# Expert attention of a two-layer token model: the order of TensorE's work within a pair, and gates one pair earlier

## Chip, cores and metric

The kernel runs on one core of one Trainium2 chip. The metric is the device time of one execution in microseconds (us). The kernel before takes 2606.87 us, the median of three runs (2605.61 to 2609.41).

## What is computed

The model takes 128 images through a tokenizer, two attention and feed-forward layers, and an expert layer. The change lies in the first feed-forward part, here called expert attention. Cut to what matters, it computes for `x` of 128 images, 64 tokens and 256 features:

```python
xn = layernorm(x) * norm_w
gate = softmax(xn @ router_w.T + router_b)          # 4 experts
xc = xn.reshape(B, T, C, DC)                        # 4 chunks of 64 features
q, k, v = einsum('btcd,ekd->btcek', xc, qkv_w)      # per chunk, expert and head (2 heads of 32)
attn = softmax(einsum('bcehtd,bcehsd->bcehts', q, k) * scale)
y = einsum('bcehts,bcehsd->bcehtd', attn, v)
y = einsum('btced,eod->btceo', y, proj_w) + proj_b
out = einsum('btceo,bte->btco', y, gate).reshape(B, T, D)
x = x + out @ out_w.T
```

All of it is in float32.

## The kernel before, in words

**Tiling.** Two images make a pair of 128 rows; there are 64 pairs, numbered p. The stream of activations, `h2`, stays on chip. Four pairs make a block, which is normalized and transposed together (class `Block`, 16 of them); what belongs to a single pair is in class `Pair`. The projection of each expert is folded into the values' weights, so a pair needs queries, keys, values, scores, softmax, the product with the values and one output product.

**Steps of a pair.** On TensorE: `queries_keys` (L1014, 64 matmuls in two halves, 64x64 tiles of the array), `values` (L1034, 64 matmuls in two halves, 64x64), `scores` (L1059, 128 matmuls, 32x64), the transposes of the attention weights (L1096, 16, 128x128), `mixed`, the product of values and weights (L1109, 64, 128x64), and `output` (L1125, 4, 128x128). On VectorE: `maxima` (L1069), `less_max` (L1073), `sums` with a reciprocal (L1079, L1080), half of the values' copies out of PSUM (L1048) and `added`, which adds the output product to the stream (L1129). On ScalarE: the copies of queries and keys (L1020), of the transposed weights (L1099), of `mixed` (L1120), of the other half of the values (L1046), and the exponents (L1076). On GpSimd: `weights`, a small product of reciprocal sums and gates (L1086) and a large one with the exponents (L1087).

**Three pairs at once.** The loop in `rest` handles three pairs in iteration p: `cur` (p) from its scores to its weights, `old` (p-1) from the transposes of its weights to the addition, and `new` (p+1), whose queries, keys and values are made. Pair 0 runs beside the end of the previous stage in `first`.

**Steps of a block.** These are spread over the iterations before the block's first pair n by a table, `work`, keyed by iteration and place. `at(...)` fills it and `do((p, place))` writes out what stands there. They are the statistics on VectorE ("DVE", at n-11 and n-10); on GpSimd ("POOL") the factors (L885 to L897, nine small operations, at n-9) and one normal with its stream each (L913 and L921, at n-8 to n-5); the transposes (L936) with their ScalarE copies; the logits of the router (L956, its copy L966, its transpose L971); and the gates' softmax (L976 to L988), which ends in `gates` on GpSimd.

**What sets the order.** The whole stage stands in a `manual_schedule`, so each engine runs its instructions in the order in which they are written; an instruction waits for what it reads and for the buffer it writes. PSUM has two areas here. One, `pss`, has two buffers of two banks for the scores (`sc`). The other, `sh.ps`, is one ring of four one-bank buffers that all other products share in order.

Of the kernel before, what the change touches and what calls it, by code (L numbers as in the profile page):

```python
# [12 lines left out]
F32 = mybir.dt.float32  # L13
# [7 lines left out]
P = 128  # L21
B = 128
T = 64
D = 256
# [266 lines left out]
class Shared:  # L291
# [13 lines left out]
    def ps(self, shape, name):  # L305
        return self.psq.tile(shape, F32, tag="pq", name=name)
# [455 lines left out]
def expert_attention(c, sh, front, hd, normw, wr, br, wqkv, wvT, wproj, bproj, wout):  # L762
# [4 lines left out]
    tc, nc, h2 = c.tc, c.nc, c.h2  # L767
# [3 lines left out]
    ps, small = sh.ps, sh.small  # L771
# [64 lines left out]
    wt = Weights()  # L836
# [15 lines left out]
    class Block:  # L852
# [4 lines left out]
        def __init__(self, p0):  # L857
            self.p0 = p0
            self.b = p0 // NB
# [78 lines left out]
        def transposed(self, fc):  # L938
            if fc == 0:
                self.xT = row(self.b)[:, NB * D :].rearrange("p (c n t) -> p c n t", c=2, n=NB)  # L940
            nc.scalar.activation(self.xT[:, fc], self.pt, AF.Copy, scale=nw[:, fc : fc + 1])
# [48 lines left out]
    class Pair:  # L990
# [4 lines left out]
        def __init__(self, p, blk):  # L995
            self.p, self.n, self.blk = p, p % NB, blk
            self.xT = blk.xT[:, :, p % NB, :]
            self.e, self.sm, self.pT = {}, {}, {}
            self.v = None

            qk = ring(sh.bp, "k", [P, 2, 16, T])
            self.qk = qk.rearrange("p (c a e t) -> p c a e t", c=4, a=2, e=2)

        def queries_keys(self, fc):

            self.pq = pq = [ps([P, 2, 2, P], "pqk") for _ in range(2)]
            for k in range(2):
                for eh in range(2):
                    for half in range(2):
                        o = slice(half * 64, half * 64 + 64)  # L1010
                        for par in range(2):
                            r = slice(par * 64, par * 64 + 64)
                            f = k * D + eh * P + half * 64
                            nc.tensor.matmul(  # L1014
                                pq[par][o, k, eh, :], wt.w[r, f : f + 64], self.xT[r, fc], start=True, stop=True
                            )

        def queries_keys_copied(self, fc, copy=nc.scalar.copy, pars=range(2)):
            for par in pars:
                copy(self.qk[:, 2 * fc + par], self.pq[par])  # L1020

        def values(self, h):

# [62 lines left out]
            eng.tensor_mul(s2, s2, bcast(self.blk.gate[:, self.n, x::2], 1, 8))  # L1086
            eng.tensor_mul(e, e, bcast(sm, 2, T))  # L1087

        def transposed(self, x):
            e = self.e.pop(x)  # L1090
            self.pT[x] = pT = self.pools.ep.tile([P, 2, 4, P], F32, tag="pT", name="pT")
            for h in range(2):
                pt = ps([P, 4, P], "pt")
                for cq in range(4):
                    i = h * 8 + cq * 2
                    nc.tensor.transpose(  # L1096
                        pt[:, cq, :], e[:, i : i + 2, :].rearrange("p e s -> p (e s)"), c.ident
                    )
                nc.scalar.copy(pT[:, h], pt)  # L1099

        def mixed(self):

# [48 lines left out]
    def at(n, place, f, *a):  # L1151
        key = (n, place) if n >= 0 else "first"
        work.setdefault(key, []).append(lambda: f(*a))

    for b, x in enumerate(blocks):
        n = NB * b
        if b > 2:
            at(n - 11, "DVE", x.statistics, 0)
            at(n - 10, "DVE", x.statistics, 2)
        if b > 1:  # L1160
            at(n - 9 + 2 * (b == 2), "POOL", x.factors)
            for k in range(NB):
                at((1, 2, 2, 3)[k] if b == 2 else n - 8 + k, "POOL", x.normal, k)
        elif b == 1:
            for k in range(NB):
                at(1 + k // 2, "ACT2", x.stream_scalar, k)
        if b:
            at(n - 4, "PE", x.transpose, 0)
            at(n - 3, "ACT", x.transposed, 0)
            at(n - 3, "PE", x.transpose, 1)  # L1170
            at(n - 2, "ACT", x.transposed, 1)
            at(n - 2, "PE", x.logits_in_strips)
            at(n - 1, "ACT", x.logits_copied)
            at(n - 1, "PE", x.logits_transposed)
            at(n, "DVE0", x.logits_less_max)
            at(n, "ACT1", x.exponents)
            at(n, "DVE1", x.sums)
            at(n, "POOL0", x.gates)

    def do(key):  # L1180
        for step in work.pop(key, ()):
            step()
# [7 lines left out]
    pairs = {}  # L1190
# [6 lines left out]
    x, y, z = blocks[:3]  # L1197
# [31 lines left out]
    def first(cur, new, chunk, last):  # L1229

        new.queries_keys(0)
        chunk.exponents()
        new.queries_keys_copied(0)
        chunk.sums()
        chunk.weights()
        cur.scores()
        cur.maxima(0)
        cur.less_max(0)
        y.normal_scalar(0)
        new.queries_keys(1)  # L1240
        cur.maxima(1)
        cur.less_max(1)
        chunk.transpose()
        new.queries_keys_copied(1)
        chunk.transposed()
        cur.exponents(0)
        last.outcome(0)
        last.outcome(1)
        for par in range(2):
            last.outcome_copied(0, par)  # L1250
        cur.sums(0)
        cur.weights(0)
        cur.exponents(1)
        for par in range(2):
            last.outcome_copied(1, par, nc.vector.tensor_copy)
        cur.sums(1)
        cur.weights(1)
        new.values(0)
        new.values_kept(0)
        last.back(0)  # L1260
        last.back(1)
        last.added(0)
        last.added(1)
        for k in range(1, 4):
            y.normal_scalar(k)
        new.values(1)
        new.values_kept(1)
        last.back(2)
        last.back(3)
        last.added(2)  # L1270
        last.added(3)
        sh.end.close()
        front.open()
        for k in range(NB):
            x.stream(k)
        do((0, "POOL"))
        do((0, "PE"))

    def rest(chunk, last):
        with (  # L1280
            tc.tile_pool(name="fe", bufs=4) as ep,
            tc.tile_pool(name="fps", bufs=2, space=PSUM) as pss,
            tc.manual_schedule(),
        ):
            Pair.pools = SimpleNamespace(ep=ep, pss=pss)
            old, cur = None, pairs[0]
            for p in range(NP):
                new = Pair(p + 1, blocks[(p + 1) // NB]) if p + 1 < NP else None
                if p == 0:
                    first(cur, new, chunk, last)  # L1290
                    old, cur = cur, new
                    continue
                if p == 8:
                    front.weights()
                do((p, "ACT"))
                do((p, "DVE0"))
                cur.scores()
                do((p, "DVE"))
                for x in range(2):
                    cur.maxima(x)  # L1300
                for x in range(2):
                    cur.less_max(x)
                do((p, "ACT1"))
                do((p, "DVE1"))
                do((p, "POOL0"))
                for x in range(2):
                    old.transposed(x)
                if new:
                    new.queries_keys(0)
                    new.queries_keys_copied(0, pars=(0,))  # L1310
                old.mixed()
                cur.exponents(0)
                if new:
                    new.queries_keys_copied(0, pars=(1,))
                old.mixed_copied()
                cur.sums(0)
                if new:
                    new.values(1)
                    new.queries_keys(1)
                cur.exponents(1)  # L1320
                if new:
                    new.values_kept(1)
                    new.queries_keys_copied(1)
                cur.weights(0)
                do((p, "ACT2"))
                old.output()
                if not new:
                    c.busy(ps([P, 2 * D], "idle"), wt.w, 3)
                cur.sums(1)
                cur.weights(1, nc.gpsimd if new else nc.vector)  # L1330
                do((p, "PE"))
                do((p, "POOL"))
                if new:
                    new.values(0)
                    new.values_kept(0)
                old.added()
                old, cur = cur, new
            for x in range(2):
                old.transposed(x)
            old.mixed()  # L1340
            old.mixed_copied()
            old.output()
            old.added()
        assert not work
# [1004 lines left out]
```

## Time and profile before

| what | value |
|---|---|
| median of three runs | 2606.87 us |
| profiled execution, its own time | 2605.81 us |
| its span, first to last instruction | 2604.1 us |
| mean granted TensorE clock | 0.989 |
| scores of pair 0 to scores of pair 63 | 1083.3 to 1800.4 us |
| large weights product on GpSimd (L1087) | 127 of 1902 ns |
| exponents on ScalarE (L1076) | 128 of 1062 ns |
| transposed-weight copies on ScalarE (L1099) | 256 of 599 ns |
| query and key copies on ScalarE (L1020) | 254 of 583 ns |

In the profile, PE is TensorE, DVE is VectorE, ACT is ScalarE, POOL is GpSimd, and PEld is TensorE's loading of weights. A line of the timeline holds the start in us from the first instruction, the duration, the engine, the line of the kernel, the operation, the tile written and the tiles read, the shape, and how many neighbouring instructions are merged (x32). A bracket at the end gives the engine's idle time before it and what ended it. A line of a stretch holds its length, the busy time of PE, PEld, DVE, ACT and POOL with their instruction counts, then the mean granted TensorE clock (1.00 is full speed), the share of DMA and its GB/s. Each float32 product appears as two matmul instructions, while a transpose is one.

### The profile page before, as it was taken

To read this page: it belongs to the slowest core of one execution; us is meant where nothing else is said; L and a number is where in the kernel's file an instruction comes from. 1 tells how busy PE (TensorE), PEld (TensorE's weight loads), DVE (VectorE), ACT (ScalarE), POOL (GpSimd) and SP (SyncE) were. 2 spreads that over 40 slices of the span, in tenths; PEclk is the share of its full clock that TensorE was granted. 3 is DMA by queue.
4 is the path that set the end of the run, shared out by engine and by line. 5 is a ranking of instruction groups with operands and counts; after the bars stand their busy time and mean duration, and the time that the engine had idled before them with its cause. 6 is when DMAs were issued, how large, how long until landed. Compare 5 with 4: busy or idle time off the path is not lost. (4 is left out here: it accounts for less than half of the span.)

```text
span 2604.1 us, 85832 instructions
## 1 busy us (share of the span) xinstructions
PE 2487.1 (96%) x37681; PEld 1697.3 (65%) x37681; DVE 2004.8 (77%) x3000; ACT 1632.2 (63%) x3421; POOL 1626.7 (62%) x1428
## 2 busy tenths in 40 slices
PE   8989999999999999899999999999999968999997
PEld 4554444444444444588888888887566557888886
DVE  5759999999999999888888888877567785444443
ACT  2228899898898888776776676665444533323232
POOL 3419999899898999676666676752233313454443
PEclk9999999999999999999999999999999989999998
DMA  3100000000000000000000000000344444555554
GB/s 115 33 13 1 2 2 2 2 2 1 2 2 1 2 13 2 3 29 14 25 14 25 14 24 14 24 14 26 81 101 99 94 113 178 189 189 191 192 193 133
DMA packets 138063, 141.45 MB, mean 54 GB/s; under 512 B 108002, under 2 KB 121860, under 8 KB 129871
## 3 DMA queue, kind: packets, MB, share of 16 engines
q1 hardware_dynamic: 128684, 119.48, 15.4%
q0 software_dynamic: 7648, 14.77, 1.8%
q8 instruction: 297, 4.87, 0.8%
q10 hardware_dynamic: 1344, 1.61, 0.2%
q14 instruction: 90, 0.73, 0.1%
HBM read 104.00 MB, written 32.54 MB: 52 GB/s over the span
## 5 line engine op out<-in xcount | busy, mean ns | idle before, releaser
L540 POOL TENSOR_TENSOR m<-q,k 128x1024 f32<-128x1024 f32 x384 | 719.6, 1907 | 55.4 <-PE sc L342 46.7
L532 DVE TENSOR_TENSOR m<-pc,k 128x2048 f32<-128x2048 f32 (+1 forms) x320 | 646.6, 2056 | 0.5 <-ACT q L472 0.5
L342 PE MATMUL sc<-m,wide 128*32 128x512 f32 x4096 | 520.1, 597 | 8.9 <-ACT m L541 6.6
L541 ACT ACTIVATE m<-m 128x1024 f32<-128x1024 f32 x384 | 402.4, 1049 | 20.5 <-POOL m L540 20.5
L342 PEld LDWEIGHTS sc<-m,wide 128*32 128x32 f32 x4096 | 134.7, 109 | 269.4 <-issue 157.9
L550 ACT ACTIVATE m<-k,q 128x64 f32<-128x64 f32 x1024 | 270.7, 338 | 0.9 <-DVE k L419 0.9
L1087 POOL TENSOR_TENSOR e<-e,mx 128x1024 f32<-128x1024 f32 x127 | 241.6, 1902 | 9.9
L1069 DVE TENSOR_REDUCE mx<-sc 128x16 f32<-128x1024 f32 x128 | 150.9, 1220 | 93.0 <-PE sc L1059 90.0
L2175 PE MATMUL ph<-xt,w1s 128*128 128x256 f32 x896 | 200.7, 382 | 2.1 <-DVE xt L2166 1.3
L2191 PE MATMUL po<-w2s,hT 128*128 128x256 f32 x896 | 198.0, 379 | 0.0
L2175 PEld LDWEIGHTS ph<-xt,w1s 128*128 128x128 f32 x896 | 171.0, 191 | 27.3 <-ACT hT L2179 2.0
L2191 PEld LDWEIGHTS po<-w2s,hT 128*128 128x128 f32 x896 | 168.1, 190 | 21.7
L1020 ACT COPY kr<-pqk 128x512 f32<-128x512 f32 x254 | 141.4, 583 | 56.8 <-PE pqk L1014 56.6
L1086 POOL TENSOR_TENSOR mx<-mx,gate 128x16 f32<-128x16 f32 x127 | 27.4, 215 | 235.2 <-DVE mx L1080 213.2
L1099 ACT COPY pT<-pt 128x512 f32<-128x512 f32 x256 | 132.1, 599 | 65.5 <-PE pt L1096 65.2
L1079 DVE TENSOR_REDUCE mx<-e 128x16 f32<-128x1024 f32 x128 | 155.0, 1211 | 11.4 <-ACT e L1076 9.6
L2209 POOL DMA_INDIRECT out<-y,rout x56 | 56.6, 1010 | 168.2 <-ACT hT L2179 119.2
L2179 ACT ACTIVATE hT<-ph,w1s 128x256 f32<-128x256 f32 x224 | 93.0, 470 | 98.6 <-PE ph L2175 95.1
L1073 DVE TENSOR_TENSOR e<-sc,mx 128x1024 f32<-128x1024 f32 x128 | 150.3, 1215 | 0.1
L2196 ACT ACTIVATE y<-y,gf 128x256 f32<-128x256 f32 x56 | 28.0, 507 | 195.0 <-issue 114.8
L1076 ACT ACTIVATE e<-e 128x1024 f32<-128x1024 f32 x128 | 136.0, 1062 | 1.1 <-DVE e L1073 0.7
L1109 PE MATMUL pz<-pT,vr 128*64 128x64 f32 x4096 | 134.7, 224 | 1.1 <-issue 0.7
(337 smaller groups left out, 4949.5 us busy)
## 6 DMA issues: line engine op xcount, KB each, us to landing
w1s<-in_we SPq DMA_DIRECT2D x30, 1028.0 KB
w2s<-in_we SPq DMA_DIRECT2D x30, 1024.0 KB
h<-hd SPq DMA_DIRECT2D x4, 2048.0 KB
hx<-h SPq DMA_DIRECT2D x4, 2048.0 KB
out<-h SPq DMA_DIRECT2D x4, 2048.0 KB
xt<-in_x SPq DMA_DIRECT2D x15, 512.0 KB
hd<-h SPq DMA_DIRECT2D x15, 512.0 KB
x<-hd SPq DMA_DIRECT2D x12, 512.0 KB
```

What stands on the lines that cost most here:

```text
L342: nc.tensor.matmul(dst[j : j + 32], wide[:, hf, s : s + 32], part, start=start, stop=stop)
L532: nc.vector.tensor_tensor(m, bcast(self.pq[:, hf, i : i + n], 3, T), k, ALU.max)
L540: nc.gpsimd.tensor_tensor(m, bcast(self.q[:, hf, s : s + 2], 3, T), k, ALU.subtract)
L541: nc.scalar.activation(m, m, AF.Relu)
L550: nc.scalar.activation(self.parts[i, hf][:, q], self.blk.k[:, hf, i], AF.Relu, bias=self.q[:, hf, i - NB // 2, q : q + 1], scale=-1.0,)
L1020: copy(self.qk[:, 2 * fc + par], self.pq[par])
L1069: nc.vector.tensor_reduce(mx, self.sc[x].rearrange("p h c s -> p (h c) s"), AX.X, ALU.max)
L1073: nc.vector.tensor_sub(e, self.sc[x].rearrange("p h c s -> p (h c) s"), bcast(self.sm[x], 2, T))
L1079: nc.vector.tensor_reduce(self.sm[x], self.e[x], AX.X, ALU.add)
L1087: eng.tensor_mul(e, e, bcast(sm, 2, T))
L2175: nc.tensor.matmul(ph[:, j], self.w1[:, w0 : w0 + P], self.xt[:, fc], start=(fc == 0), stop=(fc == 1))
L2191: nc.tensor.matmul(po, self.hT[:, f, r * P : r * P + P], self.w2[:, f, :], start=(f == 0), stop=(f == 7))
```

## The change

The iteration is written in another order, and four things move with it.

- The output product and the addition of a pair move one iteration later: a third pair, `older` (p-2), is carried for it.
- Queries and keys use the two-bank buffers of the scores when they are made in the loop, both halves one after the other.
- The transposes of the weights are split into the TensorE part (`transposes`) and the ScalarE copy (`transposed`), written alternately. Block work on TensorE comes right after them.
- In the table of block steps, the second transposed copy and the logits' copy are written one iteration earlier, each in the iteration of its TensorE step, and the gates' softmax moves from iteration n to n-1. GpSimd's block work (`POOL`), which was written after the weights of the pair, is now written ahead of them and behind the gates; VectorE's statistics (`DVE`) move from ahead of the maxima to the end of the iteration.

```diff
-        def queries_keys(self, fc):
-            self.pq = pq = [ps([P, 2, 2, P], "pqk") for _ in range(2)]
+        def queries_keys(self, fc, among_scores=False):
+            if among_scores:
+                pq = self.pools.pss.tile([P, 2, 2, 2, P], F32, tag="sc", name="pqk")
+                pq = [pq[:, par] for par in range(2)]
+            else:
+                pq = [ps([P, 2, 2, P], "pqk") for _ in range(2)]
+            self.pq[fc] = pq
...
-            at(n - 4, "PE", x.transpose, 0)
-            at(n - 3, "ACT", x.transposed, 0)
-            at(n - 3, "PE", x.transpose, 1)
-            at(n - 2, "ACT", x.transposed, 1)
+            for fc in range(2):
+                at(n - 4 + fc, "PE", x.transpose, fc)
+                at(n - 4 + fc, "ACT", x.transposed, fc)
             at(n - 2, "PE", x.logits_in_strips)
-            at(n - 1, "ACT", x.logits_copied)
+            at(n - 2, "ACT", x.logits_copied)
             at(n - 1, "PE", x.logits_transposed)
-            at(n, "DVE0", x.logits_less_max)
-            at(n, "ACT1", x.exponents)
-            at(n, "DVE1", x.sums)
-            at(n, "POOL0", x.gates)
+            at(n - 1, "DVE0", x.logits_less_max)
+            at(n - 1, "ACT1", x.exponents)
+            at(n - 1, "DVE1", x.sums)
+            at(n - 1, "POOL0", x.gates)
...
-                do((p, "ACT"))
-                do((p, "DVE0"))
                 cur.scores()
-                do((p, "DVE"))
                 for x in range(2):
                     cur.maxima(x)
                 for x in range(2):
                     cur.less_max(x)
+                for x in range(2):
+                    for h in range(2):
+                        old.transposes(x, h)
+                        old.transposed(x, h)
+                do((p, "PE"))
+                do((p, "ACT"))
+                do((p, "DVE0"))
+                if older:
+                    older.output()
+                old.mixed()
+                cur.exponents(0)
+                cur.exponents(1)
                 do((p, "ACT1"))
                 do((p, "DVE1"))
                 do((p, "POOL0"))
-                for x in range(2):
-                    old.transposed(x)
-                if new:
-                    new.queries_keys(0)
-                    new.queries_keys_copied(0, pars=(0,))
-                old.mixed()
-                cur.exponents(0)
-                if new:
-                    new.queries_keys_copied(0, pars=(1,))
-                old.mixed_copied()
-                cur.sums(0)
-                if new:
-                    new.values(1)
-                    new.queries_keys(1)
-                cur.exponents(1)
-                if new:
-                    new.values_kept(1)
-                    new.queries_keys_copied(1)
-                cur.weights(0)
+                do((p, "POOL"))
+                cur.sums(0)
+                cur.weights(0)
+                if older:
+                    older.added()
+                old.mixed_copied()
+                if new:
+                    for fc in range(2):
+                        new.queries_keys(fc, True)
+                        new.queries_keys_copied(fc)
+                else:
+                    c.busy(ps([P, 2 * D], "idle"), wt.w, 3)
                 do((p, "ACT2"))
-                old.output()
-                if not new:
-                    c.busy(ps([P, 2 * D], "idle"), wt.w, 3)
                 cur.sums(1)
                 cur.weights(1, nc.gpsimd if new else nc.vector)
-                do((p, "PE"))
-                do((p, "POOL"))
                 if new:
-                    new.values(0)
-                    new.values_kept(0)
-                old.added()
-                old, cur = cur, new
+                    for h in (1, 0):
+                        new.values(h)
+                        new.values_kept(h)
+                do((p, "DVE"))
+                older, old, cur = old, cur, new
```

After the loop, the transposes of the last pair, the output of the one before it, and then the rest of the last pair follow.

## The prediction, made before the changed kernel was run

> **What bounds the kernel now.** I read the page first, then the stretch of this stage alone, then one pair on TensorE, then the other engines in that pair. The stage runs 64 iterations of one loop; the scores of pairs 2 and 63 start at 1111.6 and 1800.4 us.
>
> ```profile
> PE 2487.1 (96%) x37681; PEld 1697.3 (65%) x37681; DVE 2004.8 (77%) x3000; ACT 1632.2 (63%) x3421; POOL 1626.7 (62%) x1428
> ```
> ```profile
> 1111.60:1800.40 688.80, 671.86 (x21126) 594.37 (x21122) 577.51 (x846) 482.24 (x854) 444.65 (x502) 1.00 0.07 20
> 1892.60:1896.10 3.50, 0.02 (x1) 0.00 (x0) 3.47 (x6) 2.98 (x6) 3.50 (x3) 1.00 0.00 0
> 1896.10:1899.60 3.50, 3.48 (x11) 2.95 (x12) 3.47 (x5) 2.81 (x4) 0.71 (x1) 0.52 0.36 60
> ```
> The first stretch is 61 pairs: 688.8/61 = 11.29 us a pair, TensorE busy 671.86 of 688.80, the others far less. TensorE bounds it. (The other two lines, from a later stage, are for the clock.)
>
> ```profile
> 1507.56 1.60 PE L1059 MATMUL sc<-kr 32*64 32x64 f32 x128
> 1509.08 1.97 PE L1096 MATMUL pt<-ident,e 128*128 128x128 f32 x16
> 1510.98 1.10 PE L1014 MATMUL pqk<-xnr,xTr 64*64 64x128 f32 x32
> 1512.01 2.21 PE L1109 MATMUL pz<-pT,vr 128*64 128x64 f32 x64
> 1514.15 1.10 PE L1034 MATMUL pv<-xTr,xnr 64*64 64x128 f32 x32
> 1515.08 1.05 PE L1014 MATMUL pqk<-xnr,xTr 64*64 64x128 f32 x32
> 1516.06 1.13 PE L1125 MATMUL po<-xTr,z 128*128 128x256 f32 x4
> 1517.03 0.60 PE L936 MATMUL ptx<-ident,xTr 128*128 128x128 f32 x4
> 1517.56 1.10 PE L1034 MATMUL pv<-xTr,xnr 64*64 64x128 f32 x32
> 1518.59 0.66 PE L1059 MATMUL sc<-kr 32*64 32x64 f32 x37
> ```
> One iteration, 11.03 us, without an idle bracket. Starts can be subtracted, modelled ends can't. The same 32 values matmuls take 0.93 us where the same tile shape follows (1514.15 to 1515.08) and 1.03 where another follows (1517.56 to 1518.59): 0.10 us is the price of a change of shape. There are seven changes an iteration.
>
> ```profile
> 1509.12 2.36 DVE L1069 TENSOR_REDUCE mx<-sc 128x16 f32<-128x1024 f32 x2 [0.72 <-PE sc L1059]
> 1511.39 2.35 DVE L1073 TENSOR_TENSOR e<-sc,mx 128x1024 f32<-128x1024 f32 x2
> 1513.79 1.22 DVE L1079 TENSOR_REDUCE mx<-e 128x16 f32<-128x1024 f32 x1
> ```
> ```profile
> 1403.19 1.90 POOL L1087 TENSOR_TENSOR e<-e,mx 128x1024 f32<-128x1024 f32 x1
> 1405.08 1.23 POOL L913 TENSOR_SCALAR oTr<-h,mv,rs 128x256 f32<-128x256 f32 x1
> 1406.40 1.23 POOL L921 TENSOR_SCALAR h<-h,rs,mr 128x256 f32<-128x256 f32 x1
> 1407.60 0.20 POOL L885 TENSOR_TENSOR rs<-mv,eps 128x4 f32<-128x4 f32 x1
> ...
> 1411.34 0.20 POOL L897 TENSOR_TENSOR rs<-rs,one 128x4 f32<-128x4 f32 x1
> 1411.53 0.21 POOL L988 TENSOR_TENSOR gate<-gate,gm 128x16 f32<-128x16 f32 x1
> 1412.92 0.21 POOL L1086 TENSOR_TENSOR mx<-mx,gate 128x16 f32<-128x16 f32 x1 [1.18 <-ACT e L1076]
> ```
> VectorE shows the chain behind the scores: counted from their start, maxima begin at +1.56 and both subtractions are done at +6.2. GpSimd shows the key fact: in every fourth iteration it has 6.45 us of block work (1405.08 to 1411.53: one normal with its stream, 2.5 us, and the factors, 3.9), which fits between the weights of one pair and of the next. The gates (L988) come after it and, in that trace, find their sums long done.
>
> **The order on TensorE.** After the change an iteration runs scores, transposes, block work, output of the pair before last, mixed, both queries_keys, both values. Seven changes of shape become four: transposes to keys, keys to mixed and keys to output are gone. 3 x 0.10 = 0.30 us. The wait of the output for its z (0.08 to 0.14 us, one pair in four) goes too: 0.33 us a pair. In the pair with logits in strips (128x32) two changes come back, 0.2 once in four. Over 62 pairs: 62 x 0.33 - 15 x 0.2 = 17, and about 2 us of one-time GpSimd waits early in the stage: **-19 us**. Here the Trainium skill bears on it: TensorEngine Tiling (Array Packing), Tiling Modes, says a change of mode drains the array, and TensorE: Matmul & The Clock Gate, Single matmul latency, gives about 166 ns for such a fill and drain. That would make 3 x 0.166 x 62 = 31 us (an estimate from the page). The row measures 0.10 for just this, so I take 19 and keep 31 for the range.
>
> The trace also has idle labelled "issue" on TensorE, mostly inside the scores (9.1 us in 14 cases at L1059). I keep it as is. Small matmuls now lie together before the scores; it could vanish or double (-13 to +13 us).
>
> **Does the new order wait by itself?** Offsets in a common iteration of 10.65 us: scores 0 to 1.5, transposes to 3.3, block 3.8, output 4.8, mixed 6.9, keys 8.7, values 10.65. ScalarE copies pT by 4.3 (before mixed), a block copy 5.0, exponents 5.1 to 7.35, z 7.7, four key copies 7.85 to 10.0 (1.07 us for two): ready 0.6 before the next scores. The keys' PSUM waits for the subtractions, done at 5.0 and 6.2, needed at 6.9 and 7.75. Sums on VectorE end at 7.7 and 9.5; the weights on GpSimd at 10.0 and 12.2; transposes need them at 12.2 and 13.1. Statistics, moved to the end, fill VectorE's idle time before the maxima. Nothing waits, with 0.6 to 1 us to spare: zero. The four-buffer ring serves 10 or 11 tiles an iteration instead of 14 or 15, all evacuated in time. The added step moves some 8 us later with its store on SP's queue and the loads behind it; nobody waits for those until the next stage, and in the last pair both adds still lie near the end: 0 (bounds -1 to +2).
>
> **The gates, one iteration earlier.** In iterations p = 3 mod 4 the gates now stand on GpSimd ahead of the block work, and that ahead of weights(0). They wait for a chain: the gate exponents stand on ScalarE behind both exponents (done +7.35, so +7.6), the gate sums on VectorE wait for them (done +8.05; queued behind: sums(0) and all after it), gates +8.1 to +8.3. GpSimd, idle since +1.6, only now starts its 6.45 us: done +14.8. weights(0) e runs 15.1 to 17.0, weights(1) 17.3 to 19.2 (2.16 us from one to the next). They were due at 12.2 and 13.1. The next iteration starts at 10.35 (the short logits transpose), its scores end at 11.9, and TensorE stands: first transposes 17.1 to 18.1, second 19.3 to 20.2, where 13.7 was due. **6.5 us a time.** Then it goes on at its pace: the block copy ends at 21.7, exponents 22.8 and 23.9, keys copied 26.9, scores 27.5; the weights of that pair are ready at 26.6 and 28.8 for 29.1 and 30.0. Nothing is caught up, TensorE is the bound.
>
> How often: GpSimd shows this long block before a gate 13 times in the stage (p = 3, 7 to 51). At p = 55 only the normal is left (2.5 us): weights 13.1 and 15.3, stall 2.5. At p = 59 nothing is queued, and only the later sums count: 1.3. Sum 13 x 6.5 + 3.8 = 88 us; some 3 us of "issue" idle hides in it: **+85 us**.
>
> **The clock.** A rule speaks against such a stall: TensorE: Matmul & The Clock Gate, HAM oscillation, says that an idle gap of over about 3.4 us halves the clock. The trace agrees: after 3.50 us of idle (second line of the stretches) the granted clock was 0.52 in the next 3.5 us, and eight L1505 matmuls took 3.20 us instead of 1.99 and 1.89. Here the gap is 5.2 us. By the rule, one 3.4 us window at half rate costs 1.7 us of work; but after restarting TensorE has only 0.95 us of transposes and then waits for weights(1) until 19.3, so much of the slow window lies under that wait. I take 1.0 a time, **+13 us**; bounds 0 and 2.5 (two windows), 0 to +33.
>
> **Sum**, against the profiled execution (span 2604.1, its own time 2605.8, 1.1 below the median): -19 + 85 + 13 = +79. From the median 2606.9: **2686**.
>
> **Rivals.**
> (a) Faster, 2586 (10%): GpSimd's detour stays off the path. It would have to finish its block work by about +9, as if started when idle at +1.6 (end +8.1). Against it: the gates' wait is in the written order, and the trace before keeps that order on every engine. Break-even is 19/15 = 1.3 us of stall per block; at +14.8 the work is 6 us too late. With only the late sums costing (15 x 1.3 = 19) the time would be unchanged.
> (b) Clock lost for two windows each time, "issue" idle doubled: 2686 + 20 + 13 = 2719 (12%). For it: a 7.0 us idle stretch early in the trace is followed by 6.8 us at half clock.
> (c) The keys' copies on ScalarE come late for the scores, since they stand behind the exponents and share the scores' two PSUM buffers: 0.5 us a pair, +31: 2717 (8%). Against it: 0.6 us to spare.
> (d) Stalls of 4 to 5 us, because block work runs faster or the gate chain is shorter than I walked: 2655 (10%).
>
> The likeliest, 60%: 2686. A measurement tells some 0.2% (5.2 us) from no change. Faster 0.08, same 0.02, slower 0.90; the range 2645 to 2720 leaves out (a) and half of (b) and (c).
>
> **What would show it.** Right: pairs of about 10.7 us where nothing waits; one start-to-start of about 17 in four; transposes (L1096 before) waiting for GpSimd's e for some 6 us, 13 times; gates waiting for VectorE, the block work after them; clock at 0.5 after these. Wrong: no GpSimd wait before the transposes; scores waiting for ScalarE's key copies; pairs of 11 us in spite of four changes of shape.

## The result, and the profile after

The changed kernel takes 2697.31 us (median of 4 runs, 2690.68 to 2701.89) against 2607.69 us before: ratio 1.0342, 95% interval 1.0317 to 1.0367. The predicted time was 2686. The profiled execution of the changed kernel took 2701.89 us, the longest of its four, and that of the kernel before 2605.81; so their traces lie 96 us apart, where the medians lie 90.

First the totals on the page of the changed kernel, then its stretches: the stage from the scores of pair 1 to those of pair 63, and one iteration with p = 28 (a multiple of 4). The columns are length, busy PE, PEld, DVE, ACT and POOL, and the granted clock.

```profile
PE 2507.4 (93%) x37681; PEld 1732.7 (64%) x37681; DVE 2012.0 (75%) x3000; ACT 1638.1 (61%) x3421; POOL 1624.5 (60%) x1428
```
```profile
1102.30:1896.80 794.50, 702.45 (x21471) 637.78 (x21470) 594.93 (x862) 496.22 (x868) 446.91 (x509) 0.93 0.06 17
1450.70:1468.50 17.80, 13.27 (x355) 11.96 (x352) 9.99 (x15) 8.42 (x14) 13.21 (x20) 0.81 0.01 2
```

The 62 iterations take 794.5 us where they took 700.2 (from 1100.2 to 1800.4 in the trace before); the rest of the kernel is unchanged within 1 to 2 us. So the whole difference lies in the loop. The iteration of 17.8 us has TensorE busy for 13.3 only, at a mean clock of 0.81. Here is TensorE in it:

```profile
1450.70 1.20 PE L1064 MATMUL sc<-kr 32*64 32x64 f32 x90
1452.17 0.69 PE L1064 MATMUL sc<-kr 32*64 32x64 f32 x38 [0.26 <-issue]
1456.94 1.97 PE L1100 MATMUL pt<-ident,e 128*128 128x128 f32 x8 [4.09 <-POOL e L1092]
1459.09 1.97 PE L1100 MATMUL pt<-ident,e 128*128 128x128 f32 x8 [0.18 <-POOL e L1092]
1460.86 1.06 PE L936 MATMUL ptx<-ident,oTr 128*128 128x128 f32 x4
1461.71 1.14 PE L1131 MATMUL po<-xTr,z 128*128 128x256 f32 x4
1462.78 2.08 PE L1115 MATMUL pz<-pT,vr 128*64 128x64 f32 x64
1464.79 1.98 PE L1019 MATMUL pqk<-xTr 64*64 64x128 f32 x64
1466.59 1.93 PE L1039 MATMUL pv<-xTr 64*64 64x128 f32 x64
1468.45 1.59 PE L1064 MATMUL sc<-kr 32*64 32x64 f32 x128
```

Both halves of the transposes wait for GpSimd's product L1092 of the pair before. The second half of eight takes 1.77 us from start to start, where all sixteen took 1.90 before: the clock is down. It stood at half from 1455.11 for 6.83 us:

```profile
1455.11:1461.94 6.83, 4.81 (x21) 4.42 (x22) 2.33 (x3) 2.34 (x4) 6.29 (x5) 0.50 0.01 2
```

Now GpSimd from the iteration before (its scores start at 1440.03) to those products:

```profile
1439.65 1.90 POOL L1092 TENSOR_TENSOR e<-e,mx 128x1024 f32<-128x1024 f32 x1
1448.09 0.22 POOL L988 TENSOR_TENSOR gate<-gate,gm 128x16 f32<-128x16 f32 x1 [6.54 <-DVE gm L985]
1448.29 1.23 POOL L913 TENSOR_SCALAR oTr<-h,mv,rs 128x256 f32<-128x256 f32 x1
...
1454.55 0.20 POOL L897 TENSOR_TENSOR rs<-rs,one 128x4 f32<-128x4 f32 x1
1454.69 0.21 POOL L1091 TENSOR_TENSOR mx<-mx,gate 128x16 f32<-128x16 f32 x1
1454.99 1.90 POOL L1092 TENSOR_TENSOR e<-e,mx 128x1024 f32<-128x1024 f32 x1
1456.85 0.21 POOL L1091 TENSOR_TENSOR mx<-mx,gate 128x16 f32<-128x16 f32 x1
1457.14 1.90 POOL L1092 TENSOR_TENSOR e<-e,mx 128x1024 f32<-128x1024 f32 x1
```

GpSimd stands idle for 6.54 us in front of the gates, until VectorE's sums (L985) are there; the gates start at +8.06 from the scores. Then 6.4 us of block work follow, and then the weights, without a gap. What holds VectorE is the gates' exponents on ScalarE:

```profile
1447.33 0.20 ACT L981 ACTIVATE gate<-gate 128x16 f32<-128x16 f32 x1
```
```profile
1447.56 0.17 DVE L984 TENSOR_REDUCE gm<-gate 128x4 f32<-128x16 f32 x1 [0.78 <-ACT gate L981]
```

TensorE's longest waits in the stage, first before, then after (us in total, times, longest):

```profile
PE sc L1059 <- issue: 9.1, 14, 1.4
PE pt L1096 <- issue: 1.9, 4, 0.7
```
```profile
PE pt L1100 <- POOL e L1092: 59.9, 29, 4.7
PE sc L1064 <- issue: 25.4, 24, 3.4
PE pt L1100 <- issue: 3.6, 4, 1.9
```

There are two differences, not one: the wait for GpSimd, and far more idle labelled "issue" in the scores.

### The profile page after: what moved, and what is told of

Same layout as the page of the kernel before. It is cut to its first block, busy times and chain, and to the rows that moved or that the text cites. A ratio compares the mean times of both kernels' runs of the same rounds, so it can differ in the third digit from the quotient of the medians.

```text
span 2700.1 us, 86012 instructions
## 1 busy us (share of the span) xinstructions
PE 2507.4 (93%) x37681; PEld 1732.7 (64%) x37681; DVE 2012.0 (75%) x3000; ACT 1638.1 (61%) x3421; POOL 1624.5 (60%) x1428
## 3 DMA queue, kind: packets, MB, share of 16 engines
q8 instruction: 298, 4.88, 0.7%
## 5 line engine op out<-in xcount | busy, mean ns | idle before, releaser
L1105 ACT COPY pT<-pt 128x512 f32<-128x512 f32 x256 | 137.7, 595 | 192.3 <-PE pt L1100 191.8
L1092 POOL TENSOR_TENSOR e<-e,mx 128x1024 f32<-128x1024 f32 x127 | 241.6, 1902 | 9.9
L1100 PE MATMUL pt<-ident,e 128*128 128x128 f32 x1024 | 161.4, 319 | 66.0 <-POOL e L1092 60.9
L1100 PEld LDWEIGHTS pt<-ident,e 128*128 128x128 f32 x1024 | 136.9, 164 | 79.0 <-POOL e L1092 69.3
L1025 ACT COPY kr<-pqk 128x512 f32<-128x512 f32 x254 | 130.5, 600 | 29.7 <-PE pqk L1019 29.7
```

The costliest lines, as they stand in the source:

```text
L1100: nc.tensor.transpose(pt[:, cq, :], e[:, i : i + 2, :].rearrange("p e s -> p (e s)"), c.ident)
```

## The experiments

My theory, called the queue theory: GpSimd's block work behind the waiting gates makes the weights late. Its rival, the gate-chain theory: the gates' softmax itself, now on the way of VectorE and ScalarE late in the iteration, does the harm. A second question grew out of the profile: where the "issue" idle comes from. Each ratio is to the kernel before, run again beside the experiment (2609.1 to 2610.1 us).

### GpSimd's block work behind the weights

```diff
                 do((p, "POOL0"))
-                do((p, "POOL"))
...
                 cur.weights(1, nc.gpsimd if new else nc.vector)
+                do((p, "POOL"))
```

> The changed kernel with GpSimd's block work (normals, streams, factors) written behind weights(1) of its iteration instead of ahead of weights(0). Queue theory (TensorE's long waits come from 6.45 us of block work that stands behind the waiting gates and ahead of the weights): the 13 long pairs of about 17.5 us vanish. But behind weights(1), which in those iterations end at +14, the 6.45 us reach +3.6 to +10.05 of the next iteration, 2.2 us past the time at which weights(0) is ready there; the transposes after that stand some 1.4 us, 13 times: 2607 - 19 + about 25 of added issue idle + 18 = 2631. Gate-chain theory (the wait lies in the softmax of the gates, which VectorE and ScalarE now do late in the iteration): nothing changes, 2690 to 2700.

Measured: 2612.0 us, ratio 1.0014 (1.0004 to 1.0023). The gate-chain theory falls: the gates stay where the change put them, and 85 us are back. But the time is 19 below my number. The transposes waited 5.5 us for GpSimd in all, not 18: my expectation had the block work reach weights(0) of the next iteration 2.2 us late and let all of the delay through.

### GpSimd's block work ahead of the gates

```diff
-                do((p, "POOL0"))
                 do((p, "POOL"))
+                do((p, "POOL0"))
```

> The changed kernel with two lines exchanged: GpSimd's block work stands ahead of the gates. It can then start when GpSimd is idle, at +1.6, and ends at +8.05, as the gates' sums come. Queue theory: no long pairs at all, the three changes of tile shape saved, and the larger issue idle of the changed kernel kept (29.4 us against 12.7 us before in gaps over 0.2 us, some 25 us with the short ones): 2607 - 19 + 25 = 2613, from 2600 to 2620. Gate-chain theory: 2690 to 2700. If the added issue idle comes only from the stalls and the slow clock: 2588.

Measured: 2609.8 us, ratio 1.0002 (0.9991 to 1.0013). Two lines exchanged undo the whole loss. Its GpSimd, in an iteration whose scores start at 1442.37:

```profile
1450.14 0.20 POOL L897 TENSOR_TENSOR rs<-rs,one 128x4 f32<-128x4 f32 x1
1450.97 0.21 POOL L988 TENSOR_TENSOR gate<-gate,gm 128x16 f32<-128x16 f32 x1 [0.64 <-DVE gm L985]
1452.30 0.21 POOL L1091 TENSOR_TENSOR mx<-mx,gate 128x16 f32<-128x16 f32 x1 [1.11 <-PE pv L1039]
1452.59 1.90 POOL L1092 TENSOR_TENSOR e<-e,mx 128x1024 f32<-128x1024 f32 x1
```

The block work is over before the gates' sums come. GpSimd still waits 0.64 us for the gates, and nothing that is ready stands behind them. Yet the new order brings nothing: 1.0002, although three changes of tile shape are gone. TensorE's longest waits in this kernel:

```profile
PE sc L1064 <- issue: 24.8, 25, 3.4
PE pt L1100 <- POOL e L1092: 4.1, 10, 0.5
```

So the "issue" idle doesn't come from the stalls. The price of the shapes is really saved, as an iteration without a wait shows (its next scores start at 1154.23):

```profile
1143.84 1.59 PE L1064 MATMUL sc<-kr 32*64 32x64 f32 x128
1145.37 1.97 PE L1100 MATMUL pt<-ident,e 128*128 128x128 f32 x16
1147.17 0.60 PE L936 MATMUL ptx<-ident,oTr 128*128 128x128 f32 x4
1147.60 1.03 PE L1131 MATMUL po<-xTr,z 128*128 128x256 f32 x4
1148.56 2.08 PE L1115 MATMUL pz<-pT,vr 128*64 128x64 f32 x64
1150.58 1.98 PE L1019 MATMUL pqk<-xTr 64*64 64x128 f32 x64
1152.38 1.93 PE L1039 MATMUL pv<-xTr 64*64 64x128 f32 x64
```

It takes 10.39 us, where the shortest of its class took 10.91 before (a class is the iterations of one p mod 4; this one is p = 5). For all 62 iterations I take each step from its start to the start of the next, and add up the least time of each kind of step: 672 us before, 641 here, so 31 us are saved. What the steps take beyond their least rises from 28 to 62 us, so 34 us are given back. The largest parts are:

- The scores take 19 us more, most of it the "issue" idle (24.8 us where it was 9.1).
- In four iterations (p = 10, 18, 46, 54) a wait of 1.4 to 3.4 us in the scores is followed by a half clock, which costs some 8 us. The stage before had no half clock at all. In p = 10 the sixteen transposes take 2.96 us instead of 1.90:

```profile
1202.14 0.49 PE L1064 MATMUL sc<-kr 32*64 32x64 f32 x32 [1.62 <-issue]
1202.56 3.03 PE L1100 MATMUL pt<-ident,e 128*128 128x128 f32 x16
1205.52 1.08 PE L956 MATMUL pl<-xnr,xTr 128*32 128x128 f32 x16
```
```profile
1203.25:1206.66 3.41, 3.41 (x29) 2.66 (x27) 3.41 (x4) 2.34 (x4) 0.41 (x1) 0.51 0.02 5
```

- About 6 us go where transposes with p = 0 mod 4 still wait for GpSimd's weights, and about as much where the last values with p = 3 mod 4 wait for their tile of the ring. In both, VectorE does the gates' sums first. So the gate-chain theory is right about these 12 us, though not about the loss.

### The factors twice

```diff
             at(n - 9 + 2 * (b == 2), "POOL", x.factors)
+            if b > 2:
+                at(n - 9, "POOL", x.factors)
```

> The changed kernel with the nine small GpSimd operations of the factors done twice (the same result again, 3.9 us more) in p = 3, 7 to 51, ahead of the weights. Queue theory: each of the 13 long waits grows by 3.9 us, +51, and with some more time at half clock 2748 to 2765. Gate-chain theory: no change, since GpSimd has the time: 2697.

Measured: 2747.41 us, ratio 1.0533 (1.0518 to 1.0549): 50 us above the changed kernel, 13 x 3.9 = 51. Whatever is added to GpSimd ahead of the weights is paid in full.

```profile
PE pt L1100 <- POOL e L1092: 109.8, 30, 8.5
```

### TensorE kept busy in the stall

```diff
+                if p % 4 == 0 and p < 56:
+                    c.busy(ps([P, 2 * D], "idle"), wt.w, 10)
                 for x in range(2):
                     for h in range(2):
                         old.transposes(x, h)
```

> The changed kernel with ten matmuls of 128x512 into an unread tile of the ring ahead of the transposes in every fourth iteration (p = 4 to 52), about 4.5 us of TensorE work that fits into the wait of about 5. The stall stays, the clock should stay up. Clock term as predicted (1.0 us a stall): 2697 - 13 = 2684, clock in the stage near 1.00. A window at half rate felt in full (1.7 to 3.4 us a stall): 2655 to 2675. No loss by the clock: 2697, or above it by what of the filler lies past the wait.

Measured: 2711.94 us, ratio 1.0402 (1.0386 to 1.0417). A miss of my own: each call writes two matmul instructions, so the filler was twice as long as the wait.

```profile
1454.16 8.85 PE L50 MATMUL idle<-xTr,ident 128*128 128x512 f32 x20
```

So with five calls instead of ten:

> The changed kernel with a filler of about 4.4 us (ten matmul instructions; the twenty of the run before took 8.85 us and went past the wait) ahead of the transposes in p = 4, 8 to 52. It now ends inside the wait. The long pairs stay, the clock stays up. Clock term as the trace of the changed kernel has it (second transposes 1.77 us instead of 0.95, and 0.5 us on what follows: 1.3 us a stall): 2697 - 17 = 2680. No loss by the clock: 2697. A loss of two windows in full (3.4 us a stall): 2653.

Measured: 2684.49 us, ratio 1.0287 (1.0267 to 1.0307), 12.8 us less than the changed kernel, with more work on TensorE. The clock over its stage (the number after POOL's count) is 0.99 where the changed kernel had 0.93:

```profile
1100.40:1879.30 778.90, 726.82 (x21599) 632.75 (x21598) 594.24 (x862) 491.55 (x868) 446.98 (x508) 0.99 0.06 18
```

The thirteen iterations with a stall (p = 4 to 52) fall from 17.51 to 16.14 us on the mean: 1.36 us a stall, 18 us in all, is what the clock costs. Without the stall they take 10.98 (the kernel with the two lines exchanged), so the wait itself costs 5.16. The gain of the medians is 5 us short of those 18, since other iterations lost 2 us, and the profiled execution of the changed kernel was 4.6 us above its median.

### A pause before the scores

The kernel with the block work ahead of the gates, and one product into an unread tile before the scores:

```diff
+                c.busy(ps([P, 2 * D], "idle"), wt.w, 1)
                 cur.scores()
```

> The kernel with the block work ahead of the gates (2609.8), with one 128x512 product into an unread tile (two matmul instructions, about 0.9 us by the earlier filler) ahead of the scores of every pair from 1 to 63. Supply theory (TensorE uses up its instructions in the scores faster than they are fetched, after 5.7 us of other dense small matmuls): the pause lets the fetches catch up and takes the place of much of the 46 us of excess: 2610 + 63 x 0.9 - 25 = 2641, and issue idle below 15 us. If the excess has nothing to do with how densely instructions are used: 2666 or more.

Measured: 2649.25 us, ratio 1.0146 (1.0127 to 1.0165). The excess of the iterations over the least of their class falls from 45 to 10 us (p = 4 to 59), and the scores' idle almost vanishes:

```profile
PE idle L50 <- DVE vr L1053: 13.0, 16, 0.9
PE sc L1064 <- issue: 4.9, 4, 2.8
```

The time is 8 us above my 2641: the product adds 1.06 us to the shortest iteration and not 0.9, and its tile in the ring of four waits for VectorE (13.0 us), which I hadn't counted.

The trace's records of transfers show what the "issue" idle is. The page of the changed kernel counts 298 transfers of instructions with 4.88 MB, 16 KB each. In its stage, 28 idle stretches of over 0.2 us are labelled "issue". In every one the last of these transfers landed 1.2 to 1.6 us before the end of the stretch; before the change it is the same in all 21. (Idle that ends on a semaphore shows no such rule: in the changed kernel the last landing then lies 1.5 to 6.2 us back.) Moreover, count TensorE's instructions in the trace, its sequencer's included: in both kernels the number ahead of the one that ends such a stretch is always 193 or 194 above a multiple of 256. So TensorE gets its instructions in blocks of 256, and waits there for the next block. The scores use up 256 instructions (128 matmuls and 128 loads of weights, L1064) in 1.5 us, while in none of the twelve traces do two blocks land less than 3.1 us apart.

### Smaller stores

```diff
-            n = {NP - 3: 2, NP - 2: 1, NP - 1: 1}.get(p, 4 * (p % 4 == 3))
+            n = 1
...
-            elif n == 4 and p > 3:
+            elif p % 4 == 3 and 3 < p < NP - 1:
```

On the kernel with the block work ahead of the gates:

> The kernel with the block work ahead of the gates (2609.8), with the stream stored to memory after each pair (128 KB) instead of every four (512 KB). Contention theory of the issue idle (in it the pairs with p = 2 mod 4, whose scores follow the large store and load, take 12.45 us on the mean, their least is 10.72: the fetches of instructions stand behind those transfers): that class falls to about 11, and 15 x 1.4 = 21 us go: 2589. Alignment theory (a fetch of 256 instructions is used up in the 1.5 us of the scores, whatever the data transfers do): unchanged, 2610.

On the kernel before:

> The kernel before with the stream stored after each pair instead of every four. Contention theory: the classes with excess over their least (0.37 us a pair, 23 us in all) lose a part of it: about 2600. Alignment theory: 2609, unchanged.

Measured: 2601.51 us, ratio 0.9968 (0.9955 to 0.9981), and 2604.53 us, ratio 0.9981 (0.9971 to 0.9990). In the first, the class p = 2 mod 4 falls from 12.45 to 11.61, not to 11, and the excess from 45 to 34. The size of the store explains a part of the late instructions in the new order, the smaller part (11 of the 45 us of excess). In the second the stage hardly moves (699.2 against 700.2 us); where its 5 us come from isn't settled. The first of the two is the fastest kernel of this study.

### The slow work ahead of the scores

The same four changes of shape, started elsewhere: scores, mixed, values, queries and keys, transposes, block work, output. Mixed comes a pair later, with a third buffer for the values; the gates' sums and products wait for the next iteration.

```diff
+                if older:
+                    older.mixed()
+                    older.mixed_copied()
...
+                for x in range(2):
+                    cur.exponents(x)
+                    if new:
+                        new.queries_keys(x, True)
+                        new.queries_keys_copied(x)
...
+                for x in range(2):
+                    for h in range(2):
+                        old.transposes(x, h)
+                        old.transposed(x, h)
+                do((p, "PE"))
...
+                if older:
+                    older.output()
+                    older.added()
```

> Another order with the same four changes of tile shape: scores, mixed, values, queries and keys, then transposes, block work and output at the end, directly ahead of the next scores. Mixed of a pair comes one iteration later (values in three buffers), the gates' sums and products wait until the next iteration, and GpSimd's block work stands first. The slow TensorE work (about 40 instructions in 3.3 us) now lies ahead of the scores (256 in 1.5 us), and the weights have some 5 us to spare. Supply theory: the pairs near their least of 10.4 to 10.7, issue idle below 10 us in the stage: 2607 - 21 - 15 = 2571, from 2560 to 2585. If the issue idle comes from the sum of instructions in a pair and not from their density just before the scores: as the kernel with the block work ahead of the gates, 2605 to 2612.

And with the small stores:

> The same with the stream stored after each pair. If supply now has time to spare, the size of the stores no longer matters: the same as the run beside it within 4 us. Contention theory: another 8 us less.

Measured: 2675.34 us, ratio 1.0246 (1.0232 to 1.0260), and 2673.26 us, 1.0237 (1.0219 to 1.0256). The smaller stores change 2 us, within the 4 expected. The order itself is a failure, some 100 us from my number, for two reasons that TensorE's waits in the first run show:

```profile
PE ptx L936 <- ACT pT L1108: 26.4, 29, 1.0
PE pz L1118 <- issue: 21.2, 27, 1.3
PE pl L956 <- ACT pT L1108: 13.3, 15, 1.0
PE pg L971 <- ACT pT L1108: 13.2, 15, 1.0
PE pv L1042 <- issue: 5.4, 9, 1.0
```

One is a wait that I made: the block's tile is next in the ring after the transposes' four, and their copies on ScalarE now stand behind exponents and key copies, about 0.9 us in every pair (53 us in all). The other corrects my picture of the supply. The scores no longer wait, but mixed and values do: the idle has moved to where the long run of small matmuls has used up what was fetched. The length of that run fits both orders (scores, mixed, keys and values, 640 instructions in some 7 us: a block in some 3 us, closer than any two landed), while what comes just before the scores doesn't fit the second. That the pause in the earlier run helped because it breaks the run is then likely; no run here varies the length alone.

## Why the prediction was right

**The place and the cause.** The gates' wait and the block work behind it were the step that decided, and the two exchanged lines (2609.8) and the factors written twice (2747.4) show it. In steps, counted from the scores: gates +8.06 (walked: +8.1), weights e +14.96 and +17.11 (15.1 and 17.3), transposes at +16.9 and +19.06 (17.1 and 19.3). Thirteen iterations took 16.5 to 18.3 us.

**The stall and the clock.** Walked: 85 + 13 = 98 us. Measured against the kernel with the two lines exchanged: 13 x 6.52 = 85 us, and 1.4 at p = 56, where 2.5 was walked; the small stall after p = 59 did not appear. A stall is 5.16 us of waiting, not 6.5: GpSimd was 0.2 us earlier than walked, TensorE came to the wait 0.3 later and was faster behind it (about 7.1 us from the last transposes to the next scores, not 7.3), and an iteration without a stall takes 10.98, not 10.65. So a part of rival (d), the shorter stall, came true.

The clock costs 1.36 us a stall where 1.0 was taken. The rule from the Trainium skill (TensorE: Matmul & The Clock Gate, HAM oscillation), that a gap of over about 3.4 us does it, is not what the traces show: in the changed kernel six waits of only 1.6 to 2.0 us are followed by a window of 3.41 us at half clock too. Nor was it one window: in 11 of the 13 stalls the clock stood at half for 6.83 us, as in rival (b). Much of that lies under the waits, as argued, so that it cost 1.36 and not 3.4.

**The shapes.** Walked: 19 us. Measured: 31, or 0.52 us for three changes in an iteration with p = 1 mod 4. The row read for the price, 0.93 against 1.03, holds only the end of the product ahead of a change. The product behind one starts more slowly as well: from its fourth to its fifth matmul it takes 0.14 us, and 0.09 where the shape stays. The estimate worked out from the figure of about 166 ns in the Trainium skill (TensorE: Matmul & The Clock Gate, Single matmul latency), also 31, was the better one, though it left out the changes that come back with the logits.

**The supply.** "I keep it as is" put at nothing what became the largest miss: the longer scores (19 us) and the half clock behind them (8). The range held the first as "double".

**Waits of the new order.** "Nothing waits" held for keys, scores and PSUM of the scores. It did not hold for the two waits of about 6 us each that the gates' new place brings. For the values of p = 3 mod 4, the later `added` (L1135), behind the gates' sums on VectorE, frees its ring tile late; their step takes 2.35 us instead of 1.86:

```profile
1449.67 0.85 PEld L1039 LDWEIGHTS pv<-xTr 64*64 64x64 f32 x30 [0.32 <-DVE h L1135]
```

**The sum.** In the traces the stage grew by 94 us: -31 for the shapes, +34 given back to waits and clock, +86 for the stalls with their clock, and +5 in other iterations of the changed kernel. In the medians it is 90, and 79 was predicted. So the cause and its main term were right, to some 15%. That the total came within 11 us is in part luck: the stalls were walked 12 us too dear and the saving of shapes 12 us too small, and these 24 us hid most of the 39 us of waits and slow clock (34 and 5) that were put at nothing. On the rivals: (a) fell with the changed kernel and is in effect what the two exchanged lines make of it, without its gain (its figure should read 2588, 2606.9 - 19); (c) fell; (b) and (d) each came true in part.

## What to carry to other kernels

When a step that waits is moved on an in-order engine, list what is written behind it and who needs that: here a product of 0.2 us that had to wait was written ahead of 6.4 us of ready work, and both ahead of the one result that TensorE needed. The repair is not to undo the change but to write work that is ready ahead of work that waits. And a saving on a bound engine has to be checked at that engine's next limit: grouping small matmuls saved 31 us of shape changes and lost as much again, most of it to waiting for instructions and to the slow clock behind such waits.

## What the runs showed of the hardware

TensorE can run out of instructions. They come to it in blocks of 256 (16 KB), which landed no closer than 3.1 us apart in the twelve traces. Where small instructions are used up faster than that (640 in some 7 us), it stood idle for up to 3.4 us at a time, until 1.2 to 1.6 us after a block had landed (49 of 49 stretches in the kernels before and after). About 1 us of other work per pair before the scores took the scores' idle from 24.8 to 4.9 us. The idle is labelled only "issue". As the blocks are counted off in the order of the instructions, it falls on the same pairs in different kernels (p = 18 has 3.4 us in both the changed kernel and the one with the lines exchanged).

TensorE's clock changed only on a fixed grid of 3.413 us. In this stage, over all twelve traces, every window at full clock in which TensorE was busy for less than 51% was followed by one at half clock, and none in which it was busy for more than 61% (in all 53 of 2449 such windows had a half clock behind them; the ends of matmuls are modelled, so these shares are estimates). So a wait of 1.4 to 2.0 us could be enough, where it fell well on the grid, and a wait of 3.5 to 4.7 us cost 1.36 us more than itself through the clock.
